# Last block of a two-layer graph kernel: values kept by tokens, weighted sums by quarters of the block

## The chip, the cores and the metric

The kernel runs on one core of a Trainium2 chip. A core has a matrix engine (PE, with a separate stream of weight loads), a vector engine (DVE), an activation engine (ACT), a general engine (POOL) and a queue engine (SP); each takes its instructions in the order in which they were written, and waits on semaphores for the others. The metric is the time of one execution on the device in microseconds. All data is fp32.

## The reference

Two layers over 128 graphs of 64 nodes with 768 features; the second is the one that the change touches:

```python
# layer 0: x = layernorm(x + relu(layernorm(attention over neighbours)))
# layer 1:
q, k, v = heads(x @ Wq + bq), heads(x @ Wk + bk), heads(x @ Wv + bv)    # 12 heads of 64
scores = q @ k.T / sqrt(64) + beta * adj
scores = where(adj > 0, scores, -9e15)
out = softmax(scores) @ v
x = layernorm(x + out)
```

## The kernel before

**Tiling.** The 8192 tokens are cut into 16 blocks of 512: four tiles (t = 0 to 3) of 128 tokens, each holding two graphs (g = 0, 1) of 64 nodes. A 512 x 768 x 768 product is done with seven block products (1, 2, 6, 5, 7, 4, 3) in place of eight; `seven` (L364) runs them, each for two halves j, so 14 groups of matmuls. In front of a group it calls what is hooked to its place (places 0 to 13: place 10 is in front of (4, j=0), place 13 in front of (3, j=1)); behind it, `step` takes one instruction each from three queues (`first`, `urgent`, `lazy`) of small work. So the order of each engine's instructions is written out by hand through places and queues, and no scheduler changes it.

**Layer 1 of a block.** For three head groups (hg) of four heads, `projected` makes q and k, `scores` (L814) multiplies them, masks, subtracts the maximum and takes exponentials on ACT, 16 instructions a group, each 32 rows of tokens to 32 columns of another 32-row part (L850); `turn` (L852) then transposes 32 x 32 squares on DVE, so that `eT` holds exponentials with the neighbour on the partition. A head pair (r = 0, 1) lies side by side, so after that the row half of `eT` is the head r, and the column half is the graph. `values` (L758) makes v with an added column of ones. For `weighted` (L863) v must lie with head r on the row half as well. In blocks 0 to 14 three copies on ACT swap the halves; in the last block (`in_place`) each addition out of PSUM is cut into four of 64 x 192, which write v straight to the swapped place (L773 to L777).

**The end of a block.** `weighted` multiplies per head group, 64 x 64 x 65 a time; the 65th column is the softmax's denominator. `added` (L882) takes a reciprocal, and one DVE instruction for each tile and head divides and adds 64 columns to the residual (L889). `finish_by_act` (L894) makes the layer norm's sums on ACT, with small DVE steps between, norms on ACT and stores through POOL's queue; `finish` (L943) does it with DVE statistics (L352, L353) and SP's queue.

**The tail.** Block 15 has no successor to hide behind. Its values carry as hooks block 14's `finish_by_act` (lazy queue), the third group's scores at place 4, and the weighted sums of tiles 2 and 3 for two groups at places 12 and 13 (L1152, L1153). Behind the values come the third group's sums of tiles 2 and 3, their norm by ACT, the three groups' sums of tiles 0 and 1, and their norm by DVE (L1154 to L1167).

Of the kernel before, what the change touches and what calls it, by code (L numbers as in the profile page):

```python
# [51 lines left out]
def gnn_two_layers(ctx: ExitStack, tc, x, adj, wl, bl, ws, bs, wr, br, gamma, beta,  # L52
# [68 lines left out]
    def later(key, *fs, queue=lazy):  # L121
        queue.extend((key, f) if callable(f) else (key, *f) for f in fs)
# [632 lines left out]

        return one, two

    def values(n, hooks={}, in_place=False):  # L758

        def pairs(a):
            return a.rearrange("p (j r d) -> p r j d", r=2, d=HD)

        def last(t, h, ps, part):
            add = pairs(bias["v"][:, h * HALF : (h + 1) * HALF] if part is None else part)
            heads = slice(h * 3, (h + 1) * 3)
            if not in_place:  # L770
                nc.vector.tensor_tensor(v[:, t, :, heads, 0:HD], pairs(ps), add, ALU.add)
                return
            for r in range(2):  # L773
                for g in range(2):
                    rows = slice(g * L, (g + 1) * L)
                    nc.vector.tensor_tensor(v[r * L : (r + 1) * L, t, g, heads, 0:HD],
                                            pairs(ps)[rows, r], add[rows, r], ALU.add)  # L777

        by_tokens("v", blocks[n]["S"], last, None, hooks)
        if not in_place:  # L780
            low, high = v[0:L, :, 1, :, 0:HD], v[L:P, :, 0, :, 0:HD]
            swap = l0t.tile([P, T, HP, HD], F32, tag="lr", name="swap")
            later(("v", n), act(lambda: nc.scalar.copy(swap[0:L], high)), act(lambda: nc.scalar.copy(high, low)),
                  act(lambda: nc.scalar.copy(low, swap[0:L])), queue=urgent)
# [29 lines left out]
    def scores(n, hg, at_once=1, pool=None, gaps=1):  # L814

        blk = blocks[n]
        q, k = blk["qk"]
        settle("e")  # L820
# [21 lines left out]
        def exponentials(groups):  # L842
            if 0 in groups:
                blk["eT", hg] = (pool or l1e_p).tile([P, T, 2, P], F32, tag="lr" if pool else "eT", name="eT")
            e = blk["eT", hg].rearrange("p t c i -> p (t c) i")
            for a in groups:
                rows = slice(a * Q, (a + 1) * Q)
                for b in range(P // Q):
                    cols = slice(b * Q, (b + 1) * Q)
                    nc.scalar.activation(e[cols, :, rows], pairs[rows, :, cols], AF.Exp)  # L850

        def turn(h):  # L852
            e = blk["eT", hg][:, h * 2 : h * 2 + 2].rearrange("p t c i -> p (t c i)")
# [6 lines left out]
              *[act(partial(exponentials, range(a, a + at_once))) for a in range(0, P // Q, at_once)], *[GAP] * gaps,  # L860
              *([partial(turn, 0), partial(turn, 1)] if pool is None else [lambda: (turn(0), turn(1))]), queue=urgent)

    def weighted(n, hg, halves=range(2), heads=range(2)):  # L863


        blk = blocks[n]
        settle(("v", n))
        settle(("e", n, hg))
        freed()
        xt, eT = blk["x"], blk["eT", hg]  # L870
        y = {(r, h): ps_mm.tile([P, 2, 2, HD + 1], F32, tag="mm", name=f"ps_y{r}") for h in halves for r in range(2)}
        for h in halves:
            for t in range(2):
                for c in heads:
                    for r in range(2):
                        rows = slice(r * L, (r + 1) * L)
                        for g in range(2):
                            cols = slice(g * L, (g + 1) * L)
                            nc.tensor.matmul(y[r, h][cols, t, c, :], lhsT=eT[rows, 2 * h + t, c, cols],  # L879
                                             rhs=v[rows, 2 * h + t, g, hg + c * HC, :], start=True, stop=True)  # L880

        def added(h, r):  # L882
            ps = y[r, h][:, :, heads[0] : heads[-1] + 1, :]
            rz = st.tile([P, 2, 2], F32, tag="rz1", name="rz1")[:, :, 0 : len(heads)]
            nc.vector.reciprocal(rz, ps[:, :, :, HD])
            for t in range(2):
                res = xt[2 * h + t].rearrange("p (c k r d) -> p r c k d", c=2, k=HC, r=2)
                for k, c in enumerate(heads):
                    nc.vector.scalar_tensor_tensor(res[:, r, c, hg, :], ps[:, t, k, 0:HD], rz[:, t, k : k + 1],  # L889
                                                   res[:, r, c, hg, :], ALU.mult, ALU.add)  # L890

        later(("y", n, hg), *[partial(added, h, r) for h in halves for r in range(2)], queue=first)

    def finish_by_act(n, tiles=range(T), queue=urgent):  # L894

        xt, key = blocks[n]["x"], ("f", n)
        total, nm, var, std, rstd, shift = (st.tile([P, T], F32, tag=f"f{k}", name=f"f{k}") for k in range(6))
        some = slice(tiles[0], tiles[-1] + 1)

        def sums(fs):  # L900
            if queue is lazy:
                unused = l0t.tile([P, 2, D], F32, tag="lr", name="unused")[:, 0, :]
            else:
                unused = l1s_p.tile([P, T * 4 * L], F32, tag="s", name="unused")[:, 0:D]
            for t in tiles:
                fs(t, unused)

        def mean():
            nc.vector.tensor_scalar(nm[:, some], total[:, some], -1.0 / D, None, ALU.mult)

        def variance():
            nc.vector.tensor_scalar(std[:, some], var[:, some], 1.0 / D, 1e-5, ALU.mult, ALU.add)

        def root():
            nc.scalar.activation(std[:, some], std[:, some], AF.Sqrt)

        def factors():
            nc.vector.reciprocal(rstd[:, some], std[:, some])
            nc.vector.tensor_tensor(shift[:, some], nm[:, some], rstd[:, some], ALU.mult)

        def norm(ts):
            for t in ts:
                nc.scalar.activation(xt[t], xt[t], AF.Identity, bias=shift[:, t : t + 1], scale=rstd[:, t : t + 1])

        def stored(ts):
            for t in ts:
                nc.gpsimd.dma_start(out=out_t[n, t], in_=xt[t])

        def act(f):
            return f, "act" if queue is urgent else "root"  # L930

        settle(("y", n, 0))
        settle(("y", n, 1))
        later(key, (partial(sums, lambda t, o: nc.scalar.activation(o, xt[t], AF.Identity,
                                                                    accum_out=total[:, t : t + 1])), "after"),
              GAP, GAP, tiny(mean),
              act(partial(sums, lambda t, o: nc.scalar.activation(o, xt[t], AF.Square, bias=nm[:, t : t + 1],
                                                                  accum_out=var[:, t : t + 1]))),
              GAP, GAP, tiny(variance), act(root), GAP, tiny(factors),
              *[act(partial(norm, tiles[k : k + 2])) for k in range(0, len(tiles), 2)],  # L940
              (partial(stored, tiles[0:2]), "free"), GAP, GAP, (partial(stored, tiles[2:]), "free"), queue=queue)

    def finish(n, tiles=range(T)):  # L943
        xt = blocks[n]["x"]

        def norm(t, mean, rstd):
            nc.vector.tensor_scalar(xt[t], xt[t], mean, rstd, ALU.subtract, ALU.mult)
            nc.sync.dma_start(out=out_t[n, t], in_=xt[t])

        for t, mr in zip(tiles, moments(("f", n), [xt[t] for t in tiles], 1e-5, urgent)):  # L950
            later(("f", n), partial(norm, t, *mr), queue=urgent)

# [67 lines left out]
    for n in range(NBLK):  # L1022
# [20 lines left out]
        if p >= 0:  # L1043
            one = left if not last else qk[0]
            at(one, 2, scores, p, 2, *((1,) if last else (2, None, 4)))
            at(one, 5, weighted, p, 1)
            if not last and m < DEEP:
                at(left, 13, weighted, p, 2)
                at(right, 0, finish_by_act, p)
            elif not last:  # L1050
                at(right, 1, weighted, p, 2)
                at(right, 2, finish_by_act, p)
            else:
                at(qk[1], 5, weighted, p, 2)

# [92 lines left out]
        for hg in range(NHG):  # L1148
            projected(n, hg, qk[hg])

    n = NBLK - 1
    values(n, {0: [partial(finish_by_act, n - 1, queue=lazy)], 4: [partial(scores, n, 2, 2, l0t)],  # L1152
               12: [partial(weighted, n, 0, (1,))], 13: [partial(weighted, n, 1, (1,))]}, True)  # L1153
    settle(("f", n - 1))  # L1154
    settle(("y", n, 0))
    settle(("y", n, 1))
    weighted(n, 2, (1,))
    settle(("y", n, 2))
    finish_by_act(n, range(2, 4))
    step()  # L1160
    for hg in range(NHG):
        weighted(n, hg, (0,))
        settle(("y", n, hg))
        step()
        step()
    finish(n, range(2))
    settle(("f", n))  # L1167


# [29 lines left out]
```

## Time and profile before

Three runs took 2944.04, 2947.76 and 2948.14 us, a median of 2947.76.

| | |
|---|---|
| profiled execution | 2945.44 us |
| its span, first to last instruction | 2943.7 us |
| instructions | 49954 |
| granted PE clock, mean | 0.995 |
| last PE matmul of block 15's values starts | 2919.71 us |
| last norm on DVE ends | 2939.63 us |
| 16 exponentials of block 15's third group | 2905.11 to 2911.93 us |

In the lines of the profile, a group row gives line, engine, operation, output and inputs, shapes and count, then total busy time and the mean of one in ns, then the idle time before it and who ended it. A timeline row gives start, duration, engine, line, operation and count, with idle time in brackets. The chain of waits is followed back from the last instruction; its rows give start, length and what held the end at that time. "PE ps_X L383" is a block product; "issue" is time without a visible cause. The trace counts each fp32 matmul of the program as two records.

### The profile page before, as it was taken

The numbers are of one execution on the slowest core, as the hardware profiler recorded it, in microseconds if no ns is written. First come the engines' busy times: TensorE is split into PE (matmuls) and PEld (weight loads), VectorE is DVE, ScalarE is ACT, GpSimd is POOL, SyncE is SP. The second block draws the span as 40 slices with busy tenths as digits, with TensorE's granted clock in tenths as the row PEclk, the third lists the DMA queues.
The fourth block names the chain that finished last, engine by engine and source line by source line (L and its number), as shares of the span: only waits on it lengthen the run. The fifth ranks groups of instructions, "written<-read, shape, count | busy, mean of one in ns | idle before, by whom it ended". The sixth has DMA issues, their size and how long they took to land.

```text
span 2943.7 us, 49954 instructions
## 1 busy us (share of the span) xinstructions
PE 2881.4 (98%) x17578; PEld 1935.1 (66%) x17578; DVE 1990.9 (68%) x4034; ACT 1123.3 (38%) x2114; POOL 729.8 (25%) x879
## 2 busy tenths in 40 slices
PE   8999999999999999999999999999999999999997
PEld 5557667575675856658576575766757567585685
DVE  5857777676676766767667576666767667676656
ACT  0004324344243542434434344443434424354254
POOL 3133122305123141321404124051230513313110
PEclk9999999999999999999999999999999999999998
DMA  9778786949669495775957759486694966849442
GB/s 329 222 247 266 230 247 181 266 135 284 160 193 248 138 292 152 207 237 157 277 149 231 216 168 271 138 254 188 183 262 136 287 158 196 247 136 289 139 127 90
DMA packets 440278, 613.18 MB, mean 208 GB/s; under 512 B 53584, under 2 KB 416720, under 8 KB 440032
## 3 DMA queue, kind: packets, MB, share of 16 engines
q1 hardware_dynamic: 362096, 493.57, 55.7%
q10 hardware_dynamic: 60848, 44.05, 8.1%
q0 software_dynamic: 17088, 72.37, 6.7%
q8 instruction: 143, 2.34, 0.3%
q14 instruction: 103, 0.84, 0.1%
HBM read 539.43 MB, written 77.27 MB: 209 GB/s over the span
## 4 chain that ended last, share of the span: by engine, by line
PE 90%; ACT 3%; DVE 3%; POOL 2%; DMA 2%; issue 1%; SPq 0%; DVEq 0%; ACTq 0%
PE ps_X L383 35%; PE ps_Y L383 26%; PE ps_Y L636 11%; PE ps_X L636 10%; PE ps_ctx L675 3%; ACT eT L850 2%; PE sc L832 2%; PE ps_y L879 2%; PE u L526 1%; POOL q L336 1%; ACT L850 1%; ACT uqk L801 1%; POOL q L335 0%; DVE o L889 0%; DMA bs<-in_L_gnn_b_self_dram 0%
## 5 line engine op out<-in xcount | busy, mean ns | idle before, releaser
L383 PE MATMUL ps_X<-xT,wqk 128*128 128x256 f32 x1728 | 395.9, 381 | 9.5 <-ACT uqk L801 9.5
L850 ACT ACTIVATE eT<-s 32x256 f32<-32x256 f32 x768 | 317.8, 414 | 184.7 <-DVE s L859 174.6
L383 PEld LDWEIGHTS ps_X<-xT,wqk 128*128 128x128 f32 x1728 | 325.8, 190 | 67.0 <-ACT uqk L801 16.2
L316 POOL TENSOR_TENSOR S<-hT 128x768 f32<-128x768 f32 x16 | 28.9, 1807 | 1132.9 <-PE ps_Y L383 1102.1
L383 PE MATMUL ps_Y<-S,wqk 128*128 128x256 f32 x1152 | 264.3, 379 | 0.0
L680 ACT ACTIVATE unused<-o 128x768 f32<-128x768 f32 x60 | 50.6, 844 | 499.6 <-DVE o L677 305.2
L383 PEld LDWEIGHTS ps_Y<-S,wqk 128*128 128x128 f32 x1152 | 218.9, 190 | 29.8
L437 DVE TENSOR_TENSOR lr<-ps_Y,u_deep 128x384 f32<-128x384 f32 x273 | 152.0, 557 | 107.5 <-PE ps_Y L636 81.4
L636 PE MATMUL ps_Y<-wlr,q 128*128 128x384 f32 x546 | 208.6, 491 | 0.0
L383 PE MATMUL ps_X<-wv,xT 128*128 128x384 f32 x576 | 195.0, 489 | 0.0
L801 ACT ACTIVATE uqk<-ps_X,bq 128x256 f32<-128x256 f32 x144 | 68.1, 473 | 325.1 <-PE ps_X L383 323.9
L383 PE MATMUL ps_X<-ws,hT 128*128 128x384 f32 x540 | 181.2, 490 | 2.8 <-DVE u L414 2.8
L809 DVE TENSOR_TENSOR q<-ps_Y,uqk 128x256 f32<-128x256 f32 x144 | 61.0, 423 | 178.0 <-ACT uqk L801 89.4
L889 DVE SCALAR_TENSOR_TENSOR o<-ps_y,rz,o 128x64 f32<-128x64 f32 x768 | 165.0, 277 | 6.8
L636 PE MATMUL ps_X<-wlr,q 128*128 128x384 f32 x364 | 151.0, 497 | 14.8 <-issue 6.2
L383 PEld LDWEIGHTS ps_X<-wv,xT 128*128 128x128 f32 x576 | 108.2, 190 | 80.8 <-issue 8.4
L383 PEld LDWEIGHTS ps_X<-ws,hT 128*128 128x128 f32 x540 | 103.2, 191 | 75.5 <-DVE u L414 3.4
L437 DVE TENSOR_TENSOR u_deep<-ps_X,lr 128x384 f32<-128x384 f32 x195 | 107.2, 550 | 67.4 <-PE ps_X L636 65.7
L636 PEld LDWEIGHTS ps_Y<-wlr,q 128*128 128x128 f32 x546 | 101.6, 190 | 67.2
L414 DVE TENSOR_TENSOR u<-ps_X,bv 128x384 f32<-128x384 f32 x96 | 53.4, 556 | 131.2 <-PE ps_X L383 131.2
L383 PE MATMUL ps_X<-S,wqk 128*128 128x256 f32 x576 | 138.2, 385 | 0.0
L383 PE MATMUL ps_Y<-xT,wqk 128*128 128x256 f32 x576 | 135.6, 385 | 0.0
(247 smaller groups left out, 5484.8 us busy)
## 6 DMA issues: line engine op xcount, KB each, us to landing
wlr<-lr_d SPq DMA_DIRECT2D x819, 192.0 KB, 3.4
wqk<-qk_d SPq DMA_DIRECT2D x672, 192.0 KB, 2.4
wv<-d_v SPq DMA_DIRECT2D x192, 192.0 KB, 2.9
ws<-d_s SPq DMA_DIRECT2D x180, 192.0 KB, 5.9
wv<-in_L_gnn_Wv_dram SPq DMA_DIRECT2D x144, 192.0 KB, 4.1
ws<-in_L_gnn_W_self_dram SPq DMA_DIRECT2D x135, 192.0 KB, 5.4
xa<-in_x_dram SPq DMA_DIRECT2D x64, 384.0 KB, 5.3
out_dram<-o POOLq DMA_DIRECT2D x62, 384.0 KB, 6.3
```

The lines of the kernel that those rows point to most:

```text
L383: nc.tensor.matmul(ps, lhsT=a, rhs=b, start=(c == 0 and i in (1, 2, 5)), stop=(c == len(fs) - 1), skip_group_check=True)
L414: evicted[nm] = nc.vector.tensor_tensor(u, ps, bias[nm][:, b * HALF : (b + 1) * HALF], ALU.add)
L437: nc.vector.tensor_tensor(dst, view(ps), add, ALU.add)
L636: nc.tensor.matmul(ps, lhsT=a, rhs=b, start=(k == 0 and j in (1, 2, 5)), stop=(k == len(fs) - 1), skip_group_check=True)
L675: nc.tensor.matmul(ps[g * L : (g + 1) * L, 0:HALF], lhsT=blk["aT"][:, t, g * L : (g + 1) * L], rhs=blk["lr"][t][:, g, cols], start=True, s ...
L680: nc.scalar.activation(unused(), o[t], AF.Identity, accum_out=total[:, t : t + 1])
L801: nc.scalar.activation(u, ps, AF.Identity, bias=bias["qk"[j]][:, c : c + 1])
L809: nc.vector.tensor_tensor(dst, ps, part, ALU.add)
L832: nc.tensor.matmul(sc[r][g * L : (g + 1) * L, t, c, :], lhsT=q[rows, c, tok], rhs=k[rows, c, tok], start=True, stop=True)
L850: nc.scalar.activation(e[cols, :, rows], pairs[rows, :, cols], AF.Exp)
L879: nc.tensor.matmul(y[r, h][cols, t, c, :], lhsT=eT[rows, 2 * h + t, c, cols], rhs=v[rows, 2 * h + t, g, hg + c * HC, :], start=True, stop= ...
L889: nc.vector.scalar_tensor_tensor(res[:, r, c, hg, :], ps[:, t, k, 0:HD], rz[:, t, k : k + 1], res[:, r, c, hg, :], ALU.mult, ALU.add)
```

## The change

Only the last block is touched. (1) Its v stays by tokens: one addition out of PSUM as in the other blocks, graph g on the row half, head r as an index. (2) Its exponentials are written to other 32 x 32 squares, so that after the transposition `eT` has the graph on the row half and the head r on the column half: both operands of a weighted sum then lie on the rows of graph g. (3) The weighted sums are made by quarters: tiles 0, 1 or 2, 3 (h), and the first or second six heads (c), over all three head groups, with 24 matmuls each, which write the output rows of the same graph g. Two reciprocals and two multiplications of 128 x 384 on DVE divide into a buffer (`shares`), and separate additions of 128 x 384 on POOL or DVE add that to the residual. (4) Layer norm statistics are taken on DVE by halves of the features, the first as soon as a half is complete; ACT norms tiles 3, 2 and 1, DVE tile 0, and ACT's and SP's queues store them. (5) The third group's scores move from place 4 to place 2. (6) Block 14's norm takes mean and squares in one step, ahead of the third group's exponentials on ACT, and stores through SP's queue.

```diff
     def values(n, hooks={}, stay=False):
...
-            if not in_place:
-                nc.vector.tensor_tensor(v[:, t, :, heads, 0:HD], pairs(ps), add, ALU.add)
-                return
-            for r in range(2):
-                for g in range(2):
-                    rows = slice(g * L, (g + 1) * L)
-                    nc.vector.tensor_tensor(v[r * L : (r + 1) * L, t, g, heads, 0:HD],
-                                            pairs(ps)[rows, r], add[rows, r], ALU.add)
+            nc.vector.tensor_tensor(v[:, t, :, heads, 0:HD], pairs(ps), add, ALU.add)
...
-                    nc.scalar.activation(e[cols, :, rows], pairs[rows, :, cols], AF.Exp)
+                    to = (b, a) if n < NBLK - 1 else (a // 2 * 2 + b % 2, b // 2 * 2 + a % 2)
+                    to = [slice(k * Q, (k + 1) * Q) for k in to]
+                    nc.scalar.activation(e[to[0], :, to[1]], pairs[rows, :, cols], AF.Exp)
...
-                nc.gpsimd.dma_start(out=out_t[n, t], in_=xt[t])
+                (nc.sync if ends else nc.gpsimd).dma_start(out=out_t[n, t], in_=xt[t])
...
+        if ends:
+
+            begin = (summed, "after"), GAP, (lambda: (mean(), squared()), "act"), GAP, GAP, tiny(variance), act(root),                 GAP, GAP, GAP, tiny(factors)
...
+    def quarter(h, c):
...
+        y = [ps_mm.tile([P, 2, NHG, HD + 1], F32, tag="mm", name=f"ps_y{r}") for r in range(2)]
+        for r in range(2):
+            for k in range(NHG):
+                for t in range(2):
+                    for g in range(2):
+                        rows = slice(g * L, (g + 1) * L)
+                        nc.tensor.matmul(y[r][rows, t, k, :], lhsT=blk_e[k][rows, 2 * h + t, c, r * L : (r + 1) * L],
+                                         rhs=v[rows, 2 * h + t, r, c * HC + k, :], start=True, stop=True)
...
+        def divided(r):
+            rz = small[:, 2 * h : 2 * h + 2, 32 + 8 * c + 4 * r : 32 + 8 * c + 4 * r + NHG]
+            nc.vector.reciprocal(rz, y[r][:, :, :, HD])
+            nc.vector.tensor_tensor(by_head[:, :, r], y[r][:, :, :, 0:HD],
+                                    rz[:, :, :, None].to_broadcast([P, 2, NHG, HD]), ALU.mult)
+
+        def added(t, engine):
+            res = xt[2 * h + t][:, c * HALF : (c + 1) * HALF]
+            engine.tensor_tensor(res, res, share[:, t, :], ALU.add)
...
+    def behind(h, c):
...
+        divided, added = quarter(h, c)
+        later(("q", h, c), partial(divided, 0), lambda: (divided(1), added(0, nc.gpsimd), added(1, nc.gpsimd)),
+              queue=first)
+
+    def measured(t, c):
+        nc.vector.bn_stats(stats[t][:, c, :], xt[t][:, c * HALF : (c + 1) * HALF])
...
+    def norm_by_act(t):
+        nc.scalar.activation(xt[t], xt[t], AF.Identity, bias=shift[:, t], scale=rstd[:, t])
+        nc.scalar.dma_start(out=out_t[n, t], in_=xt[t])
...
+    def before_last():
+
+        divided, added = quarter(1, 0)
+        for t in (2, 3):
+            measured(t, 1)
+        divided(0)
+        divided(1)
+        added(0, nc.gpsimd)
+        added(1, nc.vector)
+
+    values(n, {0: [partial(finish, n - 1, queue=lazy)], 2: [partial(scores, n, 2, 2, l0t)],
+               10: [partial(behind, 0, 0)], 11: [partial(behind, 1, 1)],
+               12: [freed, partial(measured, 0, 0), partial(measured, 1, 0)], 13: [before_last]}, True)
     settle(("f", n - 1))
...
+    divided, added = quarter(0, 1)
+    for t in (3, 2):
+        measured(t, 0)
+        whole(t)
+    factors(slice(2, 4))
+    divided(0)
+    inverse(slice(2, 4))
+    for t in (3, 2):
+        norm_by_act(t)
+    divided(1)
+    added(1, nc.gpsimd)
+    added(0, nc.vector)
+    for t in (0, 1):
+        measured(t, 1)
+        whole(t)
+    factors(slice(0, 2))
+    inverse(slice(0, 2))
+    nc.vector.tensor_scalar(xt[0], xt[0], mv[:, 0, 0:1], rstd[:, 0], ALU.subtract, ALU.mult)
+    nc.sync.dma_start(out=out_t[n, 0], in_=xt[0])
+    norm_by_act(1)
```

`whole` aggregates a tile's two statistics, `factors` adds the epsilon on DVE and takes the root on ACT, `inverse` takes the reciprocal and the shift on DVE.

## The prediction

> **What bounds the kernel now.** I read the page's busy table first, then the chain that ended last in order of time over the final 105 us, then the timeline of the same stretch, then the groups by line with shapes kept apart.
>
> ```profile
> PE 2881.4 (98%) x17578; PEld 1935.1 (66%) x17578; DVE 1990.9 (68%) x4034; ACT 1123.3 (38%) x2114; POOL 729.8 (25%) x879
> ...
> 2902.10 3.87 PE ps_Y L383 x12
> 2905.97 1.95 PE ps_X L383 x6
> 2907.92 0.02 issue
> 2907.94 0.57 DVE u L414
> 2908.53 0.35 DVE v L776
> ...
> 2932.47 1.04 ACT unused L937 x2
> 2933.53 1.04 ACT unused L937 x2
> ...
> 2938.36 0.68 DVE o L947
> 2939.04 0.59 DVEq L1195
> ```
>
> Until 2907.9 us PE carries the chain without a break. From there to 2939.6 it runs on DVE almost alone: 31.7 us of tail that no matmul bounds. The output transfers take 4.1 us more, to the span's end at 2943.7. The order built from the changed kernel differs from the old one only behind the first two matmul groups of the last block's values (2893 us), on every engine, so nothing before that can change but by noise.
>
> Rows that price the tail, old and new:
>
> ```profile
> L776 DVE TENSOR_TENSOR v<-ps_Y,u 64x192 f32<-64x192 f32 x24 | 8.5, 355 | 4.6 <-PE ps_Y L383 4.3
> L771 DVE TENSOR_TENSOR v<-ps_Y,u 128x384 f32<-128x384 f32 x90 | 50.1, 557 | 67.7 <-PE ps_Y L383 66.7
> L889 DVE SCALAR_TENSOR_TENSOR o<-ps_y,rz,o 128x64 f32<-128x64 f32 x768 | 165.0, 277 | 6.8
> L879 PE MATMUL ps_y<-v,eT 64*64 64x65 f32 x3072 | 60.6, 224 | 7.8 <-DVE rz L885 1.9 <-DVE eT L854 1.9 <-DVE f L918 1.8
> L526 PE MATMUL u<-hT 128*64 128x64 f32 x1536 | 49.5, 226 | 0.0
> L444 POOL TENSOR_TENSOR lr<-lr 128x384 f32<-128x384 f32 x39 | 38.9, 998 | 52.2 <-DVE u_deep L437 52.2
> ```
>
> The reader sees that four quarter-sized additions of one value product (4 x 355 ns, 1.47 us from first start to last end in the timeline) do what one 557 ns instruction does in the other blocks, and that the weighted sums are added in 64-column strips of 277 ns.
>
> **What the Trainium skill says.** The page "SBUF — State Buffer", section "SBUF: two separate sides", says that DVE and GpSimd share a port pair under an exclusive lock: a DVE operation with two SBUF inputs or in a two-port mode and a GpSimd operation exclude each other, and whichever starts second waits for the whole of the other. The trace agrees, in both directions:
>
> ```profile
> 2667.68 1.21 DVE L859 TENSOR_TENSOR s<-s,mx 128x1024 f32<-128x1024 f32 x1
> 2667.69 1.52 POOL L336 TENSOR_TENSOR q<-q,S 128x128 f32<-128x128 f32 x1
> ...
> 2690.72 0.99 POOL L450 TENSOR_TENSOR lr<-lr 128x384 f32<-128x384 f32 x1 [0.24 <-DVE lr L437]
> 2690.92 0.82 DVE L909 TENSOR_SCALAR f<-f 128x4 f32<-128x4 f32 x1 [0.34 <-ACT unused L934]
> ```
>
> POOL's 0.46 us row took 1.52 and ended 0.32 after DVE's; DVE's 0.17 us row ended just after POOL's. The page "TensorEngine Tiling (Array Packing)", section "Key Properties", says that tiles work independently and in parallel. The old weighted sums go round all four 64x64 tiles; the new ones use only the two on the diagonal. The trace shows the four at 60.6/3072 = 20 ns a matmul and a two-tile form (L526) at 49.5/1536 = 32 ns; no row shows the diagonal form.
>
> **The change, part by part.** Times below are on the profile's clock; a DVE instruction whose operands are ready starts about 0.08 us before its forerunner ends, one that reads the forerunner's result 0.03 after it (both read from the timeline).
>
> *Scores two groups earlier.* They start at 2893.1 instead of 2896.9 on PE (1.09 us, moved, not added). On DVE their eight-head chain (1.29 + 1.22 + 1.21 + 1.22 us) lies in waits for PE between 2894.2 and 2901.7. The squares of block 14's statistics now stand before the exponentials on ACT: they start when the mean is there (2898.0) and take the 4.2 us they took before, to 2902.2; the 16 exponentials (6.82 us) then end at about 2909.2 instead of 2911.9, and the two transposes (1.31 us) at 2910.6. DVE's variance instruction, which waits for the squares, is due at 2902.6 and is not late. PE finishes group (7,1) at 2909.85 (two 1.94 us groups fewer than 2913.7, same order). So PE stands 0.8 us for the transposes in front of the first quarter: a new wait, counted.
>
> *Values.* Each of the eight is one 0.557 us instruction instead of 1.47 us: 0.9 saved, six times behind 2908 us. The 48 exponentials of the last block keep count and shape and only land elsewhere: nothing.
>
> *Quarters on PE.* 24 matmuls each, 48 in the trace's count. At 20 ns a quarter is 0.97 us at best; at 32 ns it is 1.55; with no overlap at all between the two tiles it is twice that of the four-tile rate and more, say 54 ns (a 128x384 group, 1.94 us for 6 x 384 columns, gives 0.84 ns a column, times 64), so 2.6. I take 1.55, the two-tile row.
>
> *Quarters on DVE.* A quarter is two reciprocals (0.17) and two multiplications of 128x384 from PSUM, priced by L771 at 0.557: 1.5 us, against 2.95 us before (twelve times a reciprocal and four strips, 0.98 us from one start to the next, over four quarters). The additions to the residual go to POOL (six of 1.00 us) and DVE (two of 0.56). Statistics are eight of 0.535 and four aggregates of 0.21.
>
> *The run of it.* First quarter on PE 2910.6 to 2912.2; (4,0) to 2914.1; the quarter of the far half to 2915.7; (4,1) 2917.6; (3,0) 2919.5; third quarter 2921.1; (3,1) 2923.0. DVE in the built order: value (4,0) 2914.1, division of the first quarter with block 14's two small steps between (ready, ACT's root ends at 2910.7) to 2916.3, value (4,1) 2917.6 to 2918.2, second quarter to 2919.55, two statistics to 2920.5, value (3,0) to 2920.9, two statistics, held 0.3 by POOL's fourth addition, to 2922.1, third quarter to 2923.5, addition of tile 3 to 2924.1, value (3,1), half a us after PE had it, to 2924.6. From here DVE is the bound again. Last quarter on PE 2924.6 to 2926.1, under the statistics of tiles 3 and 2 (2926.15); first division 2926.8; inverse and shift 2927.1; second division 2927.8; addition of tile 0 2928.4; its statistics 2929.2. POOL's addition of tile 1, shut out by DVE's until 2928.4 and then 0.87 us (1.00 less the 0.13 that overlapped in the L336 case), ends at 2929.25, so tile 1's statistics run to 2930.05 (0.2 late). Small step, root on ACT, inverse, shift: 2930.9. DVE norms tile 0 by 2931.5, ACT tile 1 (1.0 us) by 2931.9. ACT has had its two other norms and transfer issues (0.35 each) since 2927.1 and is free at 2929.7, before the root.
>
> The last norm ended at 2939.63; it now ends at 2931.9: **7.7 us less**. Behind it lie the same two transfers of 384 KB, one now on ACT's queue (its issues take 0.32 us in the trace, SP's 0.34). Block 14's output moves from POOL's queue to SP's, behind nothing: the last weight load was issued before 2893. So the profiled execution of 2945.44 us (span 2943.7 and 1.7 around it) would become 2937.7. That execution lies 2.3 us under the median 2947.76 of the three runs (2944.04 to 2948.14); a median of new runs should fall between 2937.7 and 2940.1, and I write 2939.5.
>
> **Rivals.** *A smaller gain.* Twice an addition on POOL and one on DVE are set free by the same division; I let DVE win, since it starts 0.03 us behind it and POOL 0.07 to 0.14 (L444 at 2687.43 and 2680.60 behind ends at 2687.36 and 2680.46). If POOL wins, each holds DVE for about 1 us and the end is 2933.6: gain 6.0. With quarters of 2.6 us too it is 2935.9: gain 3.7; with 2.6 alone 5.3. Multiplications with a broadcast operand at 0.8 instead of 0.557 would alone cost 1.5. These give 2940.5 to 2944, around 2942.5. For it: two unpriced forms; against: each must go against its nearest row.
>
> *Slower: the diagonal quarters run one matmul at a time.* If the two tiles do not overlap at all and each matmul waits for the one before (224 ns by L879's mean), a quarter takes 48 x 0.224 = 10.8 us; all four lie on the path, as PE already waits for DVE or DVE for PE at each, and the end comes some 27 us later than now: 2975. From about 4 us a quarter PE decides and the gain is gone; at 5.4 it is 5.9 us slower. Against it: L526, whose two tiles also stand in turns, flows at 32 ns.
>
> *The exponentials are late.* Should the squares hold them so that transposes end 1.8 us later, the gain is 6.0 as well; that belongs to the smaller gain.
>
> **Numbers.** What a measurement of this kernel tells from no change is about 0.2%, 5.9 us. My forecast (gain 6 to 9, the upper end with quarters of 0.97 us) has 0.65; the smaller gain (2 to 5.9) 0.26; slower by the serial quarters or something unseen 0.09, of which 0.02 lies within 0.2%. A tenth of a per cent of scatter between runs moves a little from the first to the second, which I leave in these. Range: from 2944.04 less 8.5 to 2948.1 less 3.7, so 2935.5 to 2944.5. Faster 0.65, same 0.28, slower 0.07.
>
> **What would show it.** Right: exponentials of block 15's third group end near 2909, PE's first quarter starts within 1 us of 2910.6, a quarter takes 1 to 1.7 us, the value instruction takes 0.56 us, the last PE matmul ends near 2926, POOL's addition of tile 1 lasts beyond 1 us beside a DVE addition of 0.56, the span is near 2936. Wrong: a quarter above 3 us, a DVE addition of 1.5 us beside POOL, or an idle DVE between 2923 and 2931.

## The result, and the profile after

| | before | after |
|---|---|---|
| median, 15 runs each in turns on one chip | 2948.77 us (2943.17 to 2951.77) | 2941.15 us (2939.03 to 2943.42) |
| ratio, 95% interval | | 0.9975 [0.9967, 0.9983] |
| profiled execution | 2945.44 us | 2941.49 us |
| its span | 2943.7 us | 2939.8 us |

The median fell by 7.6 us, and the interval of the ratio stands for 5.0 to 9.7 us. The forecast was 2939.5 us with a range of 2935.5 to 2944.5; the measured median lies in the range, 1.65 us above the forecast. The two profiled executions are only 3.9 us apart, and the spans too. That gap between 7.6 and 3.9 has to be explained as well as the gain.

First the part of the page with the busy times, for the changed kernel.

```profile
PE 2879.3 (98%) x17578; PEld 1933.0 (66%) x17578; DVE 1980.6 (67%) x3973; ACT 1120.7 (38%) x2107; POOL 734.4 (25%) x879
```

DVE has 61 instructions and 10.3 us less, POOL 4.6 us more; PE's count is the same. Up to the start of block 15's values the counts of all engines are equal; behind it DVE is busy for 27.8 us instead of 38.5, and POOL for 6.65 instead of 3.25. The timeline there shows the steps of the prediction one by one (start, duration, engine, line, operation; idle time before it in brackets):

```profile
2909.55 0.56 DVE L769 TENSOR_TENSOR v<-ps_Y,u 128x384 f32<-128x384 f32 x1
...
2910.09 1.30 DVE L849 STREAM_TRANSPOSE eT<-eT 128x512 f32<-128x512 f32 x2
...
2910.79 1.62 PE L1162 MATMUL ps_y<-v,eT 64*64 64x65 f32 x48
...
2924.29 0.56 DVE L1177 TENSOR_TENSOR o<-o,shares 128x384 f32<-128x384 f32 x1
2924.34 1.37 POOL L1177 TENSOR_TENSOR o<-o,shares 128x384 f32<-128x384 f32 x1 [2.05 <-DVE shares L1172]
...
2925.37 1.50 PE L1162 MATMUL ps_y<-v,eT 64*64 64x65 f32 x44 [1.28 <-DVE v L769]
...
2928.59 0.56 DVE L1177 TENSOR_TENSOR o<-o,shares 128x384 f32<-128x384 f32 x1
2928.64 1.36 POOL L1177 TENSOR_TENSOR o<-o,shares 128x384 f32<-128x384 f32 x1 [2.93 <-DVE shares L1172]
...
2931.59 0.67 DVE L1240 TENSOR_SCALAR o<-o,small 128x768 f32<-128x768 f32 x1
2931.76 1.03 ACT L1204 ACTIVATE o<-o,small 128x768 f32<-128x768 f32 x1 [0.48 <-DVE small L1201]
2932.33 0.33 SPq L1241 DMA_DIRECT2D out_dram<-o  x1
2932.82 0.34 ACTq L1205 DMA_DIRECT2D out_dram<-o  x1
```

One value product takes one instruction of 0.56 us. A quarter takes PE 1.62 us. Twice DVE and POOL are set free by the same division, DVE starts 0.05 us ahead, and POOL's addition, 1.00 us when it is alone, takes 1.37 and ends 0.86 us after DVE's. The last norm ends at 2932.79. All this is nearly as forecast. What follows is not. The windows view (the columns behind the length are the busy times of PE, PEld, DVE, ACT and POOL, then granted clock, DMA share and GB/s):

```profile
2930.00:2935.00 5.00, 0.00 (x0) 0.00 (x0) 1.86 (x6) 1.73 (x3) 0.00 (x0) 0.56 0.76 294
2935.00:2936.00 1.00, 0.00 (x0) 0.00 (x0) 0.00 (x0) 0.00 (x0) 0.00 (x0) 0.50 0.14 52
2936.00:2939.80 3.80, 0.00 (x0) 0.00 (x0) 0.00 (x0) 0.00 (x0) 0.00 (x0) 0.50 0.00 0
```

In the last 3.8 us of the span no engine is busy and no byte moves. The chain of waits gives a hint: it names POOL's queue at L1270, the last line of the program, where POOL's closing drain begins (the drain is the last record of an engine ahead of the barrier at which the program's engines meet). It is no more than a hint, since the row lies over the time of POOL's last addition, and the chain ends with the norm.

```profile
2928.60 1.41 POOLq L1270
...
2931.76 1.03 ACT o L1204
```

The records of that drain are in the trace, though no view adds them to busy time. In the kernel before, POOL's last work is the issue of a transfer, and SP's last two transfers follow it:

```profile
2937.66 0.54 POOL L927 DMA_DIRECT2D out_dram<-o  x1 [0.38 <-ACT o L923]
```

```profile
2939.07 0.93 SPq L948 DMA_DIRECT2D out_dram<-o  x2
```

There POOL's drain ends at 2941.11, and the end waits for SP, which is done with its waits for the transfers at 2943.0. In the changed kernel POOL's last work is an addition that ends at 2930.00; its drain ends at 2939.00, while SP was done at 2935.8. The program's closing barrier then follows at 2939.04, and the span ends at 2939.8.

From one execution to the next the start of block 15's values moves by some us, with no difference in the code ahead of it (2887.7 to 2894.6 in the profiles used here). So in all that follows, times are counted from that start: from the first matmul of those values, at 2889.04 before and 2890.06 after. "Tail" is the whole stretch from there to the span's end.

| kernel | exponentials end | last norm ends | norm to end | tail | median of runs |
|---|---|---|---|---|---|
| before | 22.90 | 50.59 | 4.10 | 54.69 | 2948.77 |
| b_again | 22.90 | 52.22 | 4.11 | 56.33 | one run |
| b_third | 22.90 | 50.61 | 4.11 | 54.72 | one run |
| b_fourth | 22.90 | 51.86 | 4.10 | 55.96 | one run |
| after | 20.00 | 42.73 | 7.00 | 49.73 | 2941.15 |
| a_again | 20.01 | 42.74 | 6.98 | 49.72 | 2941.16 |
| last_two_dve | 20.00 | 43.31 | 3.80 | 47.11 | 2938.32 |
| store_by_pool | 20.01 | 42.74 | 6.70 | 49.44 | 2941.05 |
| values_in_four | 21.40 | 46.85 | 6.99 | 53.84 | 2946.31 |
| scores_at_4 | 22.88 | 47.22 | 6.99 | 54.21 | 2946.18 |
| strips | 20.01 | 44.92 | 3.76 | 48.68 | 2940.73 |
| no_pool | 20.00 | 44.01 | 3.77 | 47.78 | 2938.78 |
| filled | 22.90 | 50.60 | 4.10 | 54.70 | 2947.39 |

The medians come in four groups, each with its own runs of the kernel before: 2948.77 for `after`; 2948.38 for `a_again`, `last_two_dve` and `store_by_pool`; 2948.06, on another chip, for `values_in_four`, `scores_at_4`, `strips` and `no_pool`; and 2948.15, on a third, for `filled`. The ratios below are against the kernel before of the same group. The changed kernel was not measured beside the last two groups, so a difference to its 2941.16 carries the difference between chips as well. The first expectations count from the first weight load of the values, 0.2 us ahead of the matmul (42.9 and 50.8 there are 42.7 and 50.6 here).

### The profile page after: what moved, and what is told of

The parts are those of the page before. It is cut to its first block, busy times and chain, and to the rows that moved or that the text cites. A ratio compares the mean times of both kernels' runs of the same rounds, so it can differ in the third digit from the quotient of the medians.

```text
span 2939.8 us, 49884 instructions
## 1 busy us (share of the span) xinstructions
PE 2879.3 (98%) x17578; PEld 1933.0 (66%) x17578; DVE 1980.6 (67%) x3973; ACT 1120.7 (38%) x2107; POOL 734.4 (25%) x879
## 4 chain that ended last, share of the span: by engine, by line
PE 90%; ACT 3%; DVE 2%; POOL 2%; DMA 2%; issue 1%; SPq 0%; POOLq 0%; ACTq 0%; DVEq 0%
PE ps_X L383 35%; PE ps_Y L383 26%; PE ps_Y L636 11%; PE ps_X L636 10%; PE ps_ctx L675 3%; ACT eT L845 2%; PE sc L825 2%; PE ps_y L874 2%; PE u L526 1%; POOL q L336 1%; ACT L845 1%; ACT uqk L793 1%; POOL q L335 0%; DMA bs<-in_L_gnn_b_self_dram 0%; DMA b_k<-in_L_gnn_Wk_dram 0%
## 5 line engine op out<-in xcount | busy, mean ns | idle before, releaser
L680 ACT ACTIVATE unused<-o 128x768 f32<-128x768 f32 x60 | 50.6, 843 | 499.5 <-DVE o L677 306.3
L884 DVE SCALAR_TENSOR_TENSOR o<-ps_y,rz,o 128x64 f32<-128x64 f32 x720 | 154.7, 277 | 6.3
```

What stands on the lines that cost most here:

```text
L680: nc.scalar.activation(unused(), o[t], AF.Identity, accum_out=total[:, t : t + 1])
```

## The experiments

**Both kernels once more.** No edit. The question is which of the numbers above belong to the kernel and which to one execution.

> The changed kernel once more. In its first trace the last norm ended 42.9 us behind the first matmul of block 15's values (7.9 us less than before), but the span ended 7.0 us behind the last norm (before: 4.1), because POOL's closing drain lasted from 2928.6 to 2939.0, 9.0 us past POOL's last addition. Theory (drain): the same again, 9.0 us within 0.3. Rival (accident of one execution): a drain of 3 to 4 us and a span near 2936.5.

> The kernel before, once more, for a second trace. Both theories expect the same arithmetic tail as in its first trace: 50.8 us from the first matmul of block 15's values to the last norm's end, and 4.1 us from there to the span's end, with POOL's closing drain over (at 2941.1 in the first trace) before the last transfer has landed. If the span is some 3 us longer than 2943.7, as the median of its runs suggests, this trace shows whether the extra lies before the values or in the end.

The changed kernel repeats: median 2941.16 us, ratio 0.9978 [0.9971, 0.9985], last norm at 42.74, 6.98 us from there to the end. The kernel before does not: its last norm ended at 52.22 in this execution, 1.63 later than in the first. The exponentials end where they did. The PE timeline of b_again shows the place:

```profile
2915.75 1.84 PE L879 MATMUL ps_y<-v,eT 64*64 64x65 f32 x16 [1.28 <-DVE v L776]
2917.52 3.60 PE L383 MATMUL ps_Y<-wv,S 128*128 128x384 f32 x6
```

The block product behind PE's wait of 1.28 us for a value takes 3.60 us; in the first execution of the kernel before it took 2.20:

```profile
2916.95 2.20 PE L383 MATMUL ps_Y<-wv,S 128*128 128x384 f32 x6
```

The windows of 5 us show what goes with it. These are the ones from 2915 to 2920, first of b_again, whose clock column reads 0.70, then of the first execution, where it reads 1.00:

```profile
2915.00:2920.00 5.00, 4.06 (x20) 2.56 (x21) 1.91 (x6) 2.97 (x6) 0.00 (x0) 0.70 0.01 3
```

```profile
2915.00:2920.00 5.00, 4.40 (x55) 2.78 (x56) 2.38 (x8) 2.62 (x6) 0.00 (x0) 1.00 0.01 3
```

**POOL's last addition given to DVE, and POOL's last work made a transfer.** If the idle end is POOL's drain, it must go when POOL's last addition comes earlier. In `last_two_dve` DVE does the four additions of the two late quarters, and POOL keeps those of the two early ones:

```diff
     def before_last():
...
-        added(0, nc.gpsimd)
+        added(0, nc.vector)
         added(1, nc.vector)
...
-    added(1, nc.gpsimd)
     added(0, nc.vector)
+    added(1, nc.vector)
```

`store_by_pool` leaves the additions and lets POOL issue the store of tile 1, so that its last work is a transfer as in the kernel before:

```diff
-        nc.scalar.dma_start(out=out_t[n, t], in_=xt[t])
+        (nc.gpsimd if t == 1 else nc.scalar).dma_start(out=out_t[n, t], in_=xt[t])
```

> Tile 2's and tile 1's second additions move from POOL to DVE, so POOL's last addition is that of tile 3's other half, some 8 us earlier. DVE gets two additions of 0.48 us each, of which 0.1 lay in a wait for POOL: the last norm ends 0.8 us later, 43.7 us behind the start of the values. Theory (the drain runs some 9 us from POOL's last addition): it is over before the transfers, the span ends 3.7 us behind the last norm instead of 7.0, and the time falls by 2.5 us, to about 0.9966 of the kernel before. Rival (the drain is not tied to the additions): the time rises by 0.8 us.

> Tile 1's store, the last transfer, goes through POOL's queue, so a transfer and no addition stands last on POOL, as in the kernel before. If the drain runs 9 us from the last addition whatever follows: no change in time within 1 us. If it runs 9 us from POOL's last instruction: the span ends near 2943, 3 us later. If a transfer as POOL's last instruction makes the drain short (2.9 us behind it, as in the kernel before): the span ends near 2937, some 2.5 us earlier.

`last_two_dve` took 2938.32 us, ratio 0.997 [0.9958, 0.9981], 2.8 us under the changed kernel's 2941.16, measured beside it. DVE's additions now stand one behind the other, and the last norm ends 0.58 us later; but only 3.80 us lie behind it. POOL's last addition ends 32.23 us after the start, its drain at 41.23: again 9.00 us, now 2.1 us ahead of the last norm, where nothing waits for it. Its windows show an end that the transfers fill but for the last us:

```profile
2931.00:2934.00 3.00, 0.00 (x0) 0.00 (x0) 0.00 (x0) 0.22 (x1) 0.00 (x0) 0.50 0.68 262
2934.00:2935.00 1.00, 0.00 (x0) 0.00 (x0) 0.00 (x0) 0.00 (x0) 0.00 (x0) 0.50 0.00 0
```

So the theory of the drain holds: at the end of the span it cost the changed kernel 3.2 us, and taking it off the end gains 2.6 us by the tail and 2.8 by the medians, as the longer chain on DVE takes 0.6 back. This version has the lowest median of all that were measured.

`store_by_pool` took 2941.05 us, ratio 0.998 [0.9972, 0.9989]: no difference to the changed kernel. By the time alone that is the first case of the expectation, 9 us from the last addition whatever follows. The trace tells otherwise, if by little: the drain ended 8.56 us after the last addition, not 9.00, and 2.43 us after the end of the issue. But the issue came late:

```profile
2930.64 1.03 ACT L1204 ACTIVATE o<-o,small 128x768 f32<-128x768 f32 x1 [0.48 <-DVE small L1201]
...
2934.45 0.56 POOL L1205 DMA_DIRECT2D out_dram<-o  x1 [5.57 <-issue]
```

The norm that it stores ended at 2931.67, and POOL's issue starts 2.78 us later, without a visible cause. The first store of POOL in the tail of the kernel before came as late, 2.79 us behind the norm it waited for, with three more queued behind it; the other 58 of the 62 stores that POOL issues for block outputs in that trace started 0.29 to 0.30 us behind theirs. What was won on the drain was lost there.

**The values in four pieces again.** `values_in_four` keeps everything else and cuts the last block's additions out of PSUM into four of 64 x 192, as the kernel before did (without its swapped places):

```diff
-            nc.vector.tensor_tensor(v[:, t, :, heads, 0:HD], pairs(ps), add, ALU.add)
+            if n < NBLK - 1:
+                nc.vector.tensor_tensor(v[:, t, :, heads, 0:HD], pairs(ps), add, ALU.add)
+                return
+            for r in range(2):
+                for g in range(2):
+                    rows = slice(g * L, (g + 1) * L)
+                    nc.vector.tensor_tensor(v[rows, t, r, heads, 0:HD], pairs(ps)[rows, r], add[rows, r], ALU.add)
```

> The changed kernel with each of the last block's eight value additions cut again into four of 64 x 192 (same v, by tokens), 1.47 us for 0.56. By the prediction's schedule, with the durations of its trace, six lie behind 2908 us, but two or three of them fall where DVE waits for PE, so the last norm ends 3.1 us later (45.8 us behind the start of the values), and the time rises by 3 us against the changed kernel, POOL's drain moving with it. If the whole 5.5 us (six times 0.92) came through, DVE would have no slack at all there; if under 1 us, the single instruction was no part of the gain.

It took 2946.31 us, ratio 0.9993 [0.9985, 1.0001], some 5 us more than the changed kernel. The last norm came at 46.85, 4.1 later, where the expectation had about 3.1. The missing us is in the exponentials' column of the table: they end 1.4 us later too. DVE's timeline shows why. Two cut values stand between the steps of the third group's scores, for which ACT waits:

```profile
2897.37 1.46 DVE L775 TENSOR_TENSOR v<-ps_Y,u 64x192 f32<-64x192 f32 x4 [0.85 <-PE ps_Y L383]
2898.86 1.22 DVE L858 TENSOR_TENSOR s<-s,add 128x1024 f32<-128x1024 f32 x1
...
2900.20 1.46 DVE L775 TENSOR_TENSOR v<-ps_Y,u 64x192 f32<-64x192 f32 x4
2901.69 1.22 DVE L859 TENSOR_REDUCE mx<-s 128x16 f32<-128x1024 f32 x1
```

So the single instruction per value product is worth about 4 us of the tail, more than any other part tried alone but the next one.

**The scores at their old place.** `scores_at_4` moves the third group's scores from place 2 back to place 4:

```diff
-    values(n, {0: [partial(finish, n - 1, queue=lazy)], 2: [partial(scores, n, 2, 2, l0t)],
+    values(n, {0: [partial(finish, n - 1, queue=lazy)], 4: [partial(scores, n, 2, 2, l0t)],
```

> The changed kernel with the third group's scores back at place 4. The exponentials end some 2.7 us later, so PE waits 3.5 us in front of the first quarter instead of 0.9. If the place decides what the schedule says, the last norm ends 2.5 to 2.7 us later (45.3 to 45.5 us behind the start of the values) and the time rises by as much. If DVE has slack behind, under 1 us.

It took 2946.18 us, ratio 0.9994 [0.9986, 1.0003], some 5 us more than the changed kernel; the last norm came 4.5 us later, where the expectation had 2.5 to 2.7. The exponentials end 2.9 us later, and the first quarter 2.5. PE waits for them in the middle of the first quarter:

```profile
2913.13 1.15 PE L1162 MATMUL ps_y<-v,eT 64*64 64x65 f32 x32 [2.27 <-DVE eT L849]
2914.21 3.79 PE L383 MATMUL ps_X<-wv,xT 128*128 128x384 f32 x6
```

The group behind the wait takes 3.79 us instead of 2.20, and the granted clock between 2915 and 2920 is 0.69: the same fall as in b_again. With its 1.6 us the lag is 4.1 us at the end of that group; the last 0.4 come behind it. So the expectation had the first part and lacked the clock. The split is read from one execution; it wasn't tried apart.

**Without the separate additions, and without POOL.** `strips` goes back to strips of 64 columns that divide and add in one instruction, 12 for each quarter, and has no work for POOL in the tail. `no_pool` keeps the change's form and gives all eight additions to DVE:

```diff
-            nc.vector.tensor_tensor(by_head[:, :, r], y[r][:, :, :, 0:HD],
-                                    rz[:, :, :, None].to_broadcast([P, 2, NHG, HD]), ALU.mult)
+            for t in range(2):
+                res = xt[2 * h + t].rearrange("p (c k r d) -> p r c k d", c=2, k=HC, r=2)
+                for k in range(NHG):
+                    nc.vector.scalar_tensor_tensor(res[:, r, c, k, :], y[r][:, t, k, 0:HD], rz[:, t, k : k + 1],
+                                                   res[:, r, c, k, :], ALU.mult, ALU.add)
...
-            engine.tensor_tensor(res, res, share[:, t, :], ALU.add)
+            pass
```

```diff
-        later(("q", h, c), partial(divided, 0), lambda: (divided(1), added(0, nc.gpsimd), added(1, nc.gpsimd)),
+        later(("q", h, c), partial(divided, 0), lambda: (divided(1), added(0, nc.vector), added(1, nc.vector)),
...
-        added(0, nc.gpsimd)
+        added(0, nc.vector)
...
-    added(1, nc.gpsimd)
     added(0, nc.vector)
+    added(1, nc.vector)
```

> The changed kernel with the quarters' sums divided and added in strips of 64 columns straight into the residual, as in the kernel before (12 instructions of 277 ns, 0.195 us apart, and two reciprocals a quarter, 2.75 us), so POOL has nothing to do in the tail. Schedule: last norm 2.5 us later than in the changed kernel (45.3 us behind the start of the values). Theory (drain): POOL's drain is over long before, so the span ends 3.8 us behind the last norm instead of 7.0, and the time comes out 0.7 us below the changed kernel's, no change that can be measured. Rival: 2.5 us slower.

> All eight additions of the quarters on DVE, none on POOL. Against the kernel with only the last two moved, the first quarter's two fall into DVE's wait for PE (2916.8 to 2918.3) and cost nothing; the second quarter's two cost 0.96 less the 0.27 us wait for POOL that goes. Schedule: last norm 1.4 us later than in the changed kernel (44.2 us behind the start of the values), span 3.8 us behind it: 1.8 us faster than the changed kernel, 0.7 slower than with two moved.

`strips` took 2940.73 us, ratio 0.9975 [0.9966, 0.9983], no difference to the changed kernel (0.9978 and 2941.16) that the runs can tell; `no_pool` took 2938.78, ratio 0.9974 [0.9964, 0.9983]. The groups with shapes kept apart show the work of the strips:

```profile
L1175 DVE SCALAR_TENSOR_TENSOR o<-ps_y,small,o 128x64 f32<-128x64 f32 x48 | 9.9, 277 | 0.3
```

In its place the changed kernel has eight divisions (4.5 us in all) and two additions of 0.56 on DVE. That puts its last norm 2.19 us ahead of that of `strips`; but the drain behind POOL's addition takes it back, 7.00 us against 3.76 at the end. The separate division and POOL's help bring nothing as the change has them. In `no_pool` the norm is 1.28 us later than in the changed kernel, the end 3.2 us shorter. Only POOL's early additions pay: `last_two_dve`, which keeps those alone, ends its last norm 0.70 us ahead of `no_pool`. That is read from one execution of each; the medians of these two, 2938.32 and 2938.78, were measured on two chips and don't tell them apart.

**The kernel before at full clock.** `b_third` and `b_fourth` are the kernel before again; `filled` puts four matmuls of 128 x 256, whose result is not used, into PE's wait ahead of the last block's first weighted sum:

```diff
+        if n == NBLK - 1 and halves == (1,) and hg == 0:
+            for k in range(4):
+                nc.tensor.matmul(y[0, 1].rearrange("p t c d -> p (t c d)")[:, 0:256], lhsT=blk["S"][1][:, k % 3, 0:P],
+                                 rhs=blk["S"][1][:, k % 3, :], start=True, stop=True)
```

> The kernel before, a third look. Theory (clock): in its values PE waits for DVE around 2914 us, and in some executions its granted clock then falls to a half for 3 to 5 us, as in the second look (six matmuls of group (3,0) in 3.60 us instead of 2.20). So the last norm ends either 50.6 us behind the start of the values, with a clock of 1.00 between 2915 and 2920, or 52.2 us with a clock near 0.7; nothing between. Rival (another cause): a different number, or 52.2 with a full clock.

> The kernel before, a fourth look: the same two values as for the third, 50.6 or 52.2 us. If at least half of the four looks show 52.2, the median of its runs holds about 1.6 us that the first profiled execution, on which the prediction's sum rests, did not have.

> The kernel before with four extra matmuls of 128 x 256 (1.7 us, their result is overwritten and used by nothing) in front of the first weighted sums of tiles 2 and 3, where PE waits 1.3 us for DVE. Theory (clock): PE shows no gap over 0.3 us there, the clock stays at 1.00 to 2920, and the last norm ends 50.6 us behind the start of the values within 0.3; the time falls by up to 1.6 us, as often as the clock fell before. Rival: the clock falls all the same, or the matmuls only delay DVE by their own 1.7 us (52.3 us with a full clock).

The profiled `b_third` had the norm at 50.61 and the clock at 1.00 from 2915 to 2920; `b_fourth` had 51.86 and 0.81. So of four profiled executions of the kernel before, two have the fall, for 1.3 and 1.6 us. In `filled` PE is busy where it waited, and the clock stays at 1.00 to 2925:

```profile
2915.00:2920.00 5.00, 4.87 (x46) 3.42 (x45) 3.06 (x8) 4.11 (x8) 0.00 (x0) 1.00 0.01 3
2920.00:2925.00 5.00, 4.35 (x73) 2.48 (x71) 4.13 (x17) 0.00 (x0) 0.00 (x0) 1.00 0.00 0
```

Its norm is at 50.60, as in the undisturbed executions, though the first weighted sum starts 1.7 us later: DVE bounds this stretch, and PE had the time. The median fell by 0.8 us, ratio 0.9995 [0.9987, 1.0003], which the measurement can't tell from nothing. Since half of the executions keep the clock without the filler too, one profile of it proves little.

The traces' own record of the clock says more than these windows. In all thirteen traces the granted clock is 1.00 or 0.50 and nothing between, and within a trace its changes lie whole multiples of 3.41 us apart. It is 0.50 from 2916.97 to 2920.38 in `b_again`, from 2918.15 to 2921.56 in `b_fourth` and from 2914.69 to 2918.10 in `scores_at_4`, one step each. In the step of 3.41 us ahead of these, block products had 0.50, 0.81 and 0.47 us of PE's time. In `before` and `b_third` the step that holds the same wait of 1.28 us is cut elsewhere; there they had 1.12 and 1.22 us, and the clock stayed. So the outcome goes with how little work falls into one step, and the wait alone doesn't decide it. How little is too little isn't shown: a step of `after` with 46 matmuls of a quarter and almost no block product kept the clock too.

## Why the prediction was right, and which step failed

By its own steps, on the common clock (the prediction's times less 2889.04):

| step | predicted | measured |
|---|---|---|
| exponentials of the third group end | 20.2 | 20.00 |
| transposes end | 21.6 | 21.34 |
| PE waits ahead of the first quarter | 0.8 us | none; it starts at 20.73 |
| value product on DVE | 0.557 us | 0.557 us |
| quarter on PE | 1.55 us | 1.62 us |
| division on DVE | 0.557 us | 0.557 us |
| POOL's addition ends after DVE's | 0.87 us | 0.86 us |
| last PE matmul ends | 37.1 | 36.8 |
| last norm ends | 42.9 | 42.73 |
| from there to the span's end | 4.1 us | 7.00 us |

- **The new wait on PE** did not come. A quarter begins with the first two head groups, whose exponentials are long transposed, and reaches the third only later. The transposes end 0.61 us into the quarter and hold nothing. That was 0.8 us too much. DVE waits for PE twice behind it (2.14 and 1.45 us, ahead of the next two values), so at first most of it came through: value (4,0) starts 0.55 us earlier than forecast, counted from the start of the values. Once DVE is the bound little is left of it, and the last norm is 0.13 us early.
- **The three unpriced forms** went with their nearest rows. The diagonal pair of tiles runs at 1.62/48 = 34 ns a matmul, against 32 for the two-tile row that I took; neither rival, the slow quarters nor the serial ones, happened. A division with a broadcast operand costs 0.557 us like any 128 x 384 from PSUM.
- **The lock** that the Trainium skill describes ("SBUF — State Buffer", section "SBUF: two separate sides": the one that starts second waits for the whole of the other) went as priced, both times with DVE first, and POOL ended 0.86 us later instead of 0.87.
- **DVE the bound** at the last quarter: PE waits 1.28 us for the last value; the forecast had 1.6.
- **The step that failed** is "Behind it lie the same two transfers": from the last norm to the end I kept the 4.1 us of the kernel before. The transfers did behave so, and with POOL's drain out of the way the end takes 3.80 us. What the sum lacked is a term for POOL: its last instruction was now an addition, and its closing drain ended 9.00 us after that addition. The term is worth 2.9 us in the profile (7.00 less 4.10), and `last_two_dve` shows that it is the drain. So the span was 2939.8 us and not near 2936, the one sign of being right that did not come, and the profiled execution took 2941.49 us and not 2937.7.

So the tail gained 4.96 us in the first pair of profiles (54.69 less 49.73), not 7.73. Against the mean of the four profiles of the kernel before, 55.4, it gained 5.7, since two of them lose 1.3 and 1.6 us to a falling clock that the changed kernel, whose PE stays busy through that stretch, did not have in either of its profiles (1.00 in each window of 5 us from 2905 to 2930). The medians say 7.6 and, in the repeat, 7.2 us, with intervals of 5.0 to 9.7 and 4.4 to 8.6; 5.7 lies inside both. The remaining 1.5 to 1.9 us are within the scatter that the start of the values has in any kernel, and no run here settles them. The forecast of 2939.5 was good because 7.7 us was right for the last norm, and because part of the 2.9 us that it missed at the end was paid by a clock that it had not in its sum either. That second part was luck.

How the parts stand, by the tail of the changed kernel: taking back the single value instruction costs 4.1 us, taking back the earlier scores 4.5, taking back the divisions and POOL's additions gains 1.05, which the medians don't show (0.4). Each was taken back alone, so they need not add up to the gain.

## What to carry to other kernels

Follow each engine to its own last instruction, not only the chain to the last store: the program ends when the slowest engine has drained, so an engine with a long drain should get its last work early and leave the late, small pieces to another, even where that makes the chain of work 0.6 us longer, as it did here for 3.2 us at the end. Compare stages from a common start inside the trace when the code ahead of it is the same, because the spans of single executions carry scatter from elsewhere. And price a moved step with what it queues behind: the scores two groups earlier cost as much work as before and won through the exponentials they set free, and 1.4 of the 4.1 us of the values in one piece came the same way.

## What the runs showed of the hardware

- POOL's closing drain ends 9.00 us after the end of POOL's last elementwise instruction (TENSOR_TENSOR) in each of the seven traces where that is its last work, whether something waits for it (`after`, `a_again`, `values_in_four`, `scores_at_4`) or not (`last_two_dve`; in `strips` and `no_pool` it is over some 90 us before the end). Behind the issue of a transfer it takes 2.4 (`store_by_pool`) to 2.9 us (the kernel before).
- A transfer on POOL's queue was issued 2.78 us (`store_by_pool`) and 2.79 us (the first of the tail in `before`) after the norm it waited for had ended, but 0.29 to 0.30 us in 58 others of `before`. The cause of the late ones is open. SP's and ACT's stores of the last block follow their norm within 0.1 us.
- A wait of PE of 1.28 us was followed by a fall of the granted clock to 0.50 for 3.41 us in two of four executions of one kernel. The Trainium skill ("TensorE: Matmul & The Clock Gate", section "Part 1: The HAM clock gate (the "warmup" mystery)") says that the window over which activity is watched runs freely, and the traces agree: the changes stand on a grid of 3.41 us that cuts the same wait differently in each execution. It also says that the slow clock comes after an idle window of about 3.4 us; here PE was busy for 1.95 us (`b_again`) and 2.15 us (`b_fourth`) of the 3.41 us ahead of the fall, so the window need not be idle throughout.
- The start of the values scatters though nothing ahead of it differs in the code: 2894.59 us in `no_pool`, 2887.67 in `b_third`. Counted by the same instructions, 3.9 of these 6.9 us are there by 219 us and 3.1 come between 1250 and 1300; from there on the two stay 6.9 apart. The second part comes where PE of `no_pool` waits three times for weights from a transfer (0.64, 0.44 and 1.21 us from 1269 to 1273), with the clock at 1.00; `b_third` has no such wait there. In the first part the granted clock differs as well. These are windows of `no_pool`, then of `b_third`:

```profile
40.00:60.00 20.00, 18.08 (x52) 10.24 (x51) 8.81 (x16) 0.00 (x0) 5.31 (x9) 0.91 0.87 312
140.00:160.00 20.00, 19.79 (x57) 11.68 (x58) 16.86 (x37) 0.20 (x1) 0.00 (x0) 0.92 1.00 310
```

```profile
40.00:60.00 20.00, 19.18 (x60) 11.09 (x59) 9.79 (x18) 0.00 (x0) 5.85 (x10) 1.00 0.90 328
140.00:160.00 20.00, 20.00 (x64) 11.79 (x63) 14.59 (x31) 0.20 (x1) 0.00 (x0) 1.00 1.01 333
```

  The transfers moved less too (312 GB/s against 328, 310 against 333), and in both windows the wait came first: PE of `no_pool` had waited 1.92 us until 53.89 when the clock fell at 54.38, and it was in a wait of 2.77 us when the clock fell at 139.71. The clock alone is not the cause of the scatter: `last_two_dve` had 0.94 and 0.88 in these windows, moved 339 and 330 GB/s, and started its values at 2887.91.
